# Four of the eleven bits of a Hadamard transform: from a TensorE product with 16×16 blocks to sums and differences of row chunks on VectorE

## The chip, the cores and the metric

The kernel runs on one core of a Trainium2 chip. A core has five engines, each with its own queue of instructions that it works off in order: TensorE (PE in the profile; its weight loads are PEld), VectorE (DVE), ScalarE (ACT), GpSimd (POOL) and SyncE (SP, which here only issues DMAs). They wait for each other by semaphores. TensorE reads SBUF and writes PSUM; eight PSUM banks are used. The metric is the time of one execution on the device in microseconds (us). Everything is computed in fp32; one fp32 product is two TensorE instructions in the trace.

## The reference

Four sequences of 512 rows with 512 columns go through a gated linear scan and then through a feed-forward network, each between two layer norms and with a residual. What matters here is the second half:

```python
up_gate = jnp.einsum('bsd,hd->bsh', x, W1)
up_lin = jnp.einsum('bsd,hd->bsh', x, W3)
hidden = jax.nn.silu(up_gate) * up_lin
hidden = fwht(hidden)               # Walsh-Hadamard, 2048 values, times 1/sqrt(2048)
out = jnp.einsum('bsh,dh->bsd', hidden, W2)
```

`hidden` has 2048 columns. The transform is a symmetric 2048×2048 matrix of plus and minus ones, the Kronecker product of eleven 2×2 matrices, one for each bit of the column number.

## The kernel before

**The transform goes into the weights.** Because the transform is linear, the kernel never transforms `hidden`. It transforms the rows of w2 (2048×512) once and multiplies the untransformed `hidden` with the result. It does so in two steps. `transform_high` (line 639): rows are loaded as `(p r)`, so that partition p holds rows 16p to 16p+15, and a product with the 128×128 Hadamard matrix `h_sb` does the seven bits of p for each of 16 values of r; ScalarE copies each result back into the piece (line 644), and GpSimd's queue stores the piece in a DRAM scratch `w2_h` (line 646). `load_w2` loads it in eight pieces of two values of r; odd pieces lie in buffers of the pool `stream2`, even ones in buffers of the tag `ht`. `transform_low` (line 661): `load_low(m)` fetches rows back so that 128 consecutive rows lie on 128 partitions, and a product with `h16_sb`, a block-diagonal matrix of eight 16×16 Hadamard matrices, does the four low bits. It handles a tile m (0 to 7, two blocks of 128 rows, one of the top half of the rows and one of the bottom half) as two products of 512 columns, `g` in the profile (line 672), each followed by a scaled eviction by ScalarE (line 673).

**Seven products instead of eight.** Every matrix product is done by Winograd's form of Strassen's scheme on 2×2 blocks: seven products in the order P1, P2, P6, P5, P7, P3, P4 (`ORDER`, line 31). The sums of blocks are formed beforehand on VectorE: `combine_left` (line 124) makes S1 to S4, `combine_right` (line 131) makes T1 to T4, four operations each. P6 needs S2 and T2, P5 needs S1 and T1, P7 needs S3 and T3, P3 needs S4, P4 needs T4. A combined weight tile has seven blocks of 128×256 (896 KB over the partitions). `kept` (line 138) stores it in DRAM through GpSimd's queue, and later sequences load it from there (`again`, line 147).

**Units and filling.** The work is a row of units. `attn_unit(b, u)` with u = 0, 1, 2 does three projections of sequence b for the scan, `ffn_unit(b, m)` with m = 0 to 7 does 128 columns of both halves of w1 and w3 and makes `ht`, one eighth of `hidden`. Each unit is seven products (`project`, line 424), written into three PSUM banks X, Y and Z: P1, P6, P7 and P4 add up in X, P2 goes to Y, P5 and P3 to Z. ScalarE copies P1, P6, P5 and P4 out, VectorE adds Y after P2, X after P7 and Z after P3 (`seven`, line 392). Between the products of a unit, `run` (line 101) takes one step from the queue `fill`: after P2, P5, P3 and P4, or after every product where the unit is `dense`. The steps are products of other work: `attn_out(b)` (with the weight `wo`, tile names y, and with the gated output `og` as the left side), `ffn_out(b, part)` (with w2, tile names po; a part is two tiles m), the transposes of the next input, and here the `h` and `g` products of w2's transform. The ffn units of the first sequence are dense.

**Order on the engines.** TensorE's and SP's queues are in the order in which the program is written (line 82). The queues of VectorE, ScalarE and GpSimd are ordered by a scheduler when the kernel is built: by priority (`URGENT`, `SOON`) and by `behind(what)`, which puts work behind an earlier instruction. For each unit of the first sequence `combine_weights` makes S1 to S4 of the next unit's w1 and w3 on VectorE (eight operations), behind the unit's P7.

**Buffers.** `stream` has five buffers and holds wi, wf, wg, w1 and w3. `stream2` has four, taken in turn by pieces 1, 3, 5, 7 of w2, then `wo` (two tiles, first for sequence 0, then loaded again for sequence 1) and the tiles of w2. A load waits on SP's queue until the earlier user of its buffer is done, and every later load on that queue waits with it. For the first sequence too, w2's transformed tiles are stored and then loaded again, by `load_down_w` (line 550).

Of the kernel before, what the change touches and what calls it, by code (L numbers as in the profile page):

```python
# [11 lines left out]
F32 = mybir.dt.float32  # L12
AF = mybir.ActivationFunctionType
ALU = mybir.AluOpType
P = 128
# [11 lines left out]
S3 = A21  # L27
B11, B21, B22, B12, T1, T2, T4 = range(7)
T3 = B12

ORDER = (
    ("P1", A11, B11, "X", True),
# [10 lines left out]
def kernel(  # L43
# [14 lines left out]
    nc = tc.nc  # L58
# [2 lines left out]
    NT = T // P  # L61
    ND = D // P
    NF = FF // P
    NU = NF // 2
    NS = 2
    H = T // 2
# [18 lines left out]
    def bank(name):  # L85
        return psum.tile([P, 2, H], F32, tag="ps", name=name)
# [44 lines left out]
    def combine_right(t, eng):  # L131

        eng.tensor_sub(t[:, T1], t[:, B12], t[:, B11])
        eng.tensor_sub(t[:, T2], t[:, B22], t[:, T1])
        eng.tensor_sub(t[:, T3], t[:, B22], t[:, B12])
        eng.tensor_sub(t[:, T4], t[:, B21], t[:, T2])
# [7 lines left out]
    def stream_tile(key, b, pool=stream):  # L144
        return pool.tile([P, 7, H], F32, tag="w", name="_".join(map(str, (*key, b))))
# [39 lines left out]
        ffn_w[b, m] = weight(w1, "w1", m, b), weight(w3, "w3", m, b)  # L185


    h_sb = const.tile([P, P], F32, tag="had", name="had")
    nc.sync.dma_start(out=h_sb, in_=had)
    h16_sb = const.tile([P, P], F32, tag="had16", name="had16")  # L190
    nc.gpsimd.memset(h16_sb, 0.0)
    gn_sb = const.tile([P, ND], F32, tag="gn", name="gn")

    def load_constants():
        nc.gpsimd.dma_start(out=gn_sb, in_=gnorm.rearrange("(c p) -> p c", p=P))
        for g in range(P // 16):
            nc.gpsimd.dma_start(out=h16_sb[ts(g, 16), ts(g, 16)], in_=had[0:16, 0:16])

    ident = const.tile([P, P], F32, tag="ident", name="ident")
    make_identity(nc, ident)  # L200
# [10 lines left out]
    def behind(what):  # L211


        return tc.issue_after(read[what].ins)
# [339 lines left out]
    def ffn_out(b, part):  # L554

        ms = range(part * NS, (part + 1) * NS)
        w = {m: down_w.pop((b, m)) for m in ms}

        def multiply(ps, a, bb, first):
            if b not in outs:  # L560
                outs[b] = work.tile([P, 2, 2, D], F32, tag="wide", name=f"f_{b}", bufs=3)
            for t in range(2):
                for m in ms:
                    nc.tensor.matmul(  # L564
                        ps[:, t, :], hts[b, m][:, a, ts(t, P)], w[m][:, bb, :],
                        start=first and t == 0 and m == ms[0], stop=m == ms[-1],
                        skip_group_check=True,
                    )

        norm = {}  # L570

        end = b == B - 1 and ms[-1] == NU - 1
        held = []

        def done(i, j, tile=None):
            if not norm:
                norm[0] = OutputNorm(b, outs[b], EPS, "f")
            with tc.high_priority(offset=SOON * i):
                norm[0].quarter(i, j, (0, 1) if tile is None else (tile,))
            if j == 1 - i and tile != 0:  # L580
                norm[0].half(i, held if end else None)
                if end and i == 0:
                    return
                if end:
                    with tc.issue_after(norm[0].last.ins):
                        for residual in held:
                            residual()
                for t in range(0 if end else 2 * i, 2 * i + 2):
                    if b < B - 1:
                        eng = nc.gpsimd  # L590
                    else:
                        eng = nc.scalar if t == NT - 2 else nc.sync
                    eng.dma_start(out=out[b, ts(t, P), :], in_=xs[b][:, t, :])

        return seven(
            f"po_{b}_{part}", multiply, lambda i, j: outs[b][:, i, :, ts(j, H)],
            done if ms[-1] == NU - 1 else None, add=part > 0, by_tile=end,
        )
# [19 lines left out]
            combine_right(w[c], nc.vector)  # L618
            kept(("wo", c), w[c])

    NR = FF // P
    NJ = NR // 2
    w2_h = scratch.tile([P, NR, D], F32, tag="w2h", name="w2_h")
    w2_p = []

    def load_w2(pieces):
        for j in pieces:
            if j % 2:
                t = stream2.tile([P, 2, D], F32, tag="w", name=f"w2p_{j}")
            else:  # L630
                t = work.tile([P, 2, D], F32, tag="ht", name=f"w2p_{j}", bufs=4)
            for k in ((0, 1), (1, 2)) if j == 0 else ((0, 2),):
                nc.sync.dma_start(
                    out=t[:, k[0] : k[1], :],
                    in_=w2.rearrange("(p r) f -> p r f", r=NR)[:, 2 * j + k[0] : 2 * j + k[1], :],
                )
            w2_p.append(t)

    def transform_high(j, k):

        p = psum.tile([P, D], F32, tag="ps", name=f"h_{j}_{k}")
        t = w2_p[j]
        nc.tensor.matmul(p, h_sb, t[:, k, :], start=True, stop=True)  # L643
        nc.scalar.copy(t[:, k, :], p)  # L644
        if k == 1:
            nc.gpsimd.dma_start(out=w2_h[:, 2 * j : 2 * j + 2, :], in_=t)

    low_w = {}

    def load_low(m):  # L650
        low_w[m] = stream_tile(("w2", m), 0, stream2)
        for n, blocks in enumerate(((B11, B12), (B21, B22))):
            row = n * (NF // 2) + m
            nc.sync.dma_start(
                out=low_w[m][:, blocks[0] : blocks[1] + 1 : blocks[1] - blocks[0]],
                in_=w2_h.rearrange("p r f -> (p r) f")[ts(row, P), :].rearrange(
                    "p (n f) -> p n f", n=2
                ),
            )

    def transform_low(m):

        def make(k):
            w = low_w[m]
            if k == 0 and m + 2 < NU:
                load_low(m + 2)
            blocks = ((B11, B12), (B21, B22))[k]
            t = w[:, blocks[0] : blocks[1] + 1 : blocks[1] - blocks[0]]  # L670
            p = bank(f"g_{m}_{k}")
            nc.tensor.matmul(p, h16_sb, t, start=True, stop=True)  # L672
            nc.scalar.mul(t, p, 1.0 / FF**0.5)
            if k == 1:
                combine_right(w, nc.vector)
                kept(("w2", m), w)

        return [partial(make, k) for k in range(2)]


    def high(j0, j1):
# [26 lines left out]
    attn_unit(0, 0, True)  # L708
    with behind("P2"):
        combine_weights(2)  # L710
    attn_unit(0, 1)
    with behind("P3"):
        with tc.high_priority(offset=URGENT):
            combine_weights(2)
        with tc.high_priority(offset=SOON):
            apply = [normalize_tiles(1, "a", i, 2, True) for i in (0, 2)]
    wo_t[0] = load_wo()
    load_attn_w(1, 0)
    while fill:
# [13 lines left out]
    load_attn_w(1, 1)  # L733
    fill.extend([None] * 3 + attn_out(0))
    attn_unit(1, 0, True)
    load_low(0)
    load_low(1)
    load_attn_w(1, 2)
    fill.extend(transform_low(0) + transform_low(1))
    attn_unit(1, 1, True)  # L740
    load_ffn_w(0, 0)
    fill.extend(transposes(0, "f"))
    attn_unit(1, 2)
    with behind("P7"):
        combine_weights()
    for b in range(B):
        last = b == B - 1
        for m in range(NU):
            if m + 1 < NU:
                load_ffn_w(b, m + 1)  # L750
            if b == 0 and m % NS == 0:
                for k in range(m + 2, min(m + 2 + NS, NU)):
                    fill.extend(transform_low(k))
            if m == 0 and not last:
                fill.extend([None] * 4 * (b > 0) + attn_out(b + 1))
            if m and m % NS == 0:
                if last and m == NU - NS:
                    fill.extend([None] * 8)
                fill.extend([None] + ffn_out(b, m // NS - 1))
            if m % NS == 1:  # L760
                load_down_w(b, m // NS)
            if m == 2 and b == 0:
                load_x(2)
            if m == 4 and b + 2 < B:
                with behind("P7"):
                    late = [normalize_tiles(b + 2, "a", i, 2, True) for i in (0, 2)]
            if m in (4, 5) and b + 2 < B:
                for t, k in enumerate((3, 5) if m == 4 else (0, 3)):
                    beside[k] = [partial(behind_copy, partial(late[m - 4], range(t, t + 1)))]
            if m == 6 and not last:  # L770
                load_fold(*((b + 2, "a") if b + 2 < B else (b + 1, "f")))
            if m == NU - 1 and not last:
                transpose_fold(*((b + 2, "a") if b + 2 < B else (b + 1, "f")))
            ffn_unit(b, m, b == 0)
            with behind("P7"):
                combine_weights()
        tail = ffn_out(b, NU // NS - 1)
# [54 lines left out]
```

## Time and profile before

| what | value |
|---|---|
| three runs | 833.66, 834.70, 837.85 us; median 834.7 us |
| the profiled execution | 833.4 us, its span from first to last instruction 831.6 us |
| TensorE | busy 814.6 us, mean granted clock 0.996 |
| VectorE / ScalarE / GpSimd | busy 459.8 / 267.9 / 69.2 us |
| `h` products, line 643 | 16 calls (32 instructions), 5.3 to 48.5 us |
| `g` products, line 672 | 16 calls (32 instructions), 96.6 to 209 us |
| evictions of `g`, line 673 | 16, 588 ns each, 9.2 us |
| HBM read / written | 125.90 / 42.99 MB |

"Busy" is the time in which an engine had an instruction running. Instructions overlap at their ends: an addition of 128×512 values on VectorE has a duration of 0.69 us, but in a row of independent ones the next starts 0.605 us after the one before; for 128×256 it is 0.42 and 0.335 us, for a 128×256 fp32 product on TensorE 0.379 us per instruction with a start every 0.216 us. In the timelines below the columns are: start in us, length in us, engine, line, operation, what it writes and reads, shapes, how many instructions are merged into the row, and in brackets the idle time before it and what ended it. In the text, "pitch" is the time from start to start.

### The profile page before, as it was taken

The page shows a single profiled execution, that of the slowest core. Times are in us where ns is not written, and L with a number is a line of the kernel's source. Part 1 is how long each engine was busy: PE and PEld are TensorE (multiplying, and loading weights), DVE is VectorE, ACT ScalarE, POOL GpSimd, SP SyncE. Part 2 cuts the span into 40 slices and gives each one's busy share as a digit, 9 for nine tenths or more (in the row PEclk, how much of TensorE's full clock was granted, in tenths as well). Part 3 has the DMA queues.
Part 4 walks back from the last instruction along what each step waited for, and adds up shares of the span by engine and source line. Part 5 has one row for each costly group of instructions (what it writes and reads, how often), then busy time and mean ns, then how long its engine had stood idle before and what let it go on. Part 6 is the DMA issues. An engine that isn't in the chain of part 4 may idle for free.

```text
span 831.6 us, 9833 instructions
## 1 busy us (share of the span) xinstructions
PE 814.6 (98%) x3728; PEld 702.2 (84%) x3728; DVE 459.8 (55%) x926; ACT 267.9 (32%) x380; POOL 69.2 (8%) x112
## 2 busy tenths in 40 slices
PE   7999999999999999999999999999999999999995
PEld 4788888888888888888888888888888888888884
DVE  5486787766547657357236645637246334524345
ACT  4554463432321135235421133425221111322111
POOL 4120111111100001002000000102000000100000
PEclk9999999999999999999999999999999999999998
DMA  9996369696978435736455533825363642625201
GB/s 334 414 399 231 99 205 360 216 398 219 374 221 304 149 118 224 291 136 258 185 145 205 156 115 127 331 98 203 122 232 101 241 177 89 228 106 205 78 11 50
DMA packets 65743, 169.54 MB, mean 204 GB/s; under 512 B 4768, under 2 KB 40224, under 8 KB 65696
## 3 DMA queue, kind: packets, MB, share of 16 engines
q1 hardware_dynamic: 56528, 125.65, 43.0%
q0 software_dynamic: 8448, 41.96, 12.6%
q10 hardware_dynamic: 720, 1.31, 0.4%
q8 instruction: 29, 0.48, 0.2%
q14 instruction: 18, 0.15, 0.1%
HBM read 125.90 MB, written 42.99 MB: 203 GB/s over the span
## 4 chain that ended last, share of the span: by engine, by line
PE 93%; DVE 4%; ACT 1%; issue 1%; DMA 0%; POOL 0%; POOLq 0%; DVEq 0%; SPq 0%; ACTq 0%
PE X_f L431 25%; PE Z_f L431 13%; PE X_po L564 13%; PE X_a L431 10%; PE Z_po L564 7%; PE Y_f L431 6%; PE Z_a L431 5%; PE X_y L517 3%; PE Y_po L564 3%; PE Y_a L431 3%; PE h L643 2%; PE Z_y L517 2%; PE g L672 1%; PE Y_y L517 1%; DVE x L321 1%
## 5 line engine op out<-in xcount | busy, mean ns | idle before, releaser
L431 PE MATMUL X_f<-xt_f,w 128*128 128x256 f32 x1024 | 241.7, 379 | 0.5 <-ACT d_f L418 0.3
L431 PEld LDWEIGHTS X_f<-xt_f,w 128*128 128x128 f32 x1024 | 194.1, 190 | 30.2 <-issue 2.9
L418 ACT COPY d_f<-X_f 128x512 f32<-128x512 f32 x96 | 56.1, 584 | 294.6 <-PE X_f L431 259.3
L431 PE MATMUL Z_f<-xt_f,w 128*128 128x256 f32 x512 | 121.1, 379 | 0.2 <-ACT d_f L418 0.2
L564 PE MATMUL X_po<-w,ht 128*128 128x256 f32 x512 | 120.9, 379 | 0.2 <-DVE f L416 0.2
L431 PEld LDWEIGHTS Z_f<-xt_f,w 128*128 128x128 f32 x512 | 97.2, 190 | 15.1 <-issue 0.7
L564 PEld LDWEIGHTS X_po<-w,ht 128*128 128x128 f32 x512 | 97.2, 190 | 13.7 <-DVE f L416 0.6
L416 DVE TENSOR_TENSOR f<-X_po,f 128x512 f32<-128x512 f32 x51 | 35.2, 689 | 98.2 <-PE X_po L564 91.7
L446 DVE TENSOR_TENSOR ht<-d_f 128x1024 f32<-128x1024 f32 x32 | 39.0, 1218 | 61.2 <-ACT d_f L540 47.5
L564 PE MATMUL Z_po<-w,ht 128*128 128x256 f32 x256 | 60.5, 379 | 0.0
L431 PE MATMUL Y_f<-xt_f,w 128*128 128x256 f32 x256 | 60.5, 379 | 0.0
L431 PEld LDWEIGHTS Y_f<-xt_f,w 128*128 128x128 f32 x256 | 48.6, 190 | 7.9 <-issue 0.7
L564 PEld LDWEIGHTS Z_po<-w,ht 128*128 128x128 f32 x256 | 48.6, 190 | 6.6
L418 ACT COPY d_a<-X_a 128x512 f32<-128x512 f32 x36 | 21.0, 584 | 87.2 <-PE X_a L431 70.8
L225 POOL TENSOR_TENSOR rs_f<-rs_f,power 128x2 f32<-128x2 f32 x16 | 14.0, 878 | 405.0 <-DVE nm_f L313 383.4
L416 DVE TENSOR_TENSOR d_f<-X_f,d_f 128x512 f32<-128x512 f32 x32 | 22.1, 691 | 31.8 <-PE X_f L431 31.8
L540 ACT ACTIVATE d_f<-d_f 128x1024 f32<-128x1024 f32 x32 | 33.8, 1055 | 0.9
L431 PE MATMUL X_a<-xt_a,wi 128*128 128x256 f32 x128 | 33.1, 381 | 0.8 <-ACT w2p L644 0.7
L416 DVE TENSOR_TENSOR d_f<-Z_f,d_f 128x512 f32<-128x512 f32 x32 | 22.0, 688 | 20.6 <-PE Z_f L431 20.6
L416 DVE TENSOR_TENSOR f<-Z_po,f 128x512 f32<-128x512 f32 x28 | 19.2, 686 | 24.9 <-PE Z_po L564 24.9
L431 PE MATMUL X_a<-xt_a,wf 128*128 128x256 f32 x128 | 32.8, 379 | 0.0
L431 PEld LDWEIGHTS X_a<-xt_a,wi 128*128 128x128 f32 x128 | 23.9, 190 | 8.9 <-issue 3.1
(154 smaller groups left out, 1008.0 us busy)
## 6 DMA issues: line engine op xcount, KB each, us to landing
w<-s_w SPq DMA_DIRECT2D x80, 896.0 KB, 6.4
s_w<-w POOLq DMA_DIRECT2D x24, 896.0 KB, 6.7
w<-in_W_dram SPq DMA_DIRECT2D x32, 256.0 KB, 6.5
wi<-s_wi SPq DMA_DIRECT2D x6, 896.0 KB, 10.8
wf<-s_wf SPq DMA_DIRECT2D x6, 896.0 KB, 7.0
wg<-s_wg SPq DMA_DIRECT2D x6, 896.0 KB, 6.0
wo<-s_wo SPq DMA_DIRECT2D x6, 896.0 KB, 10.3
w_h<-w2p POOLq DMA_DIRECT2D x8, 512.0 KB, 8.2
```

Source lines behind the costliest of these rows:

```text
L225: read["power"] = nc.gpsimd.tensor_tensor(r, r, power_t[:, 0:n], ALU.pow)
L321: nc.vector.scalar_tensor_tensor(x_t, self.y[:, i, t, :], r[:, t : t + 1], x_t, ALU.mult, ALU.add)
L416: read[what] = nc.vector.tensor_add(to, ps[which], to)
L418: read["copy"] = nc.scalar.copy(to, ps[which])
L431: nc.tensor.matmul(ps[:, n, :], w[:, a, c, :], xt[:, bb, c, :], start=first and n == 0 and c == 0, stop=c == 1, skip_group_check=True,)
L446: nc.vector.tensor_mul(to.rearrange("p (t k) f -> p k t f", t=2), a.rearrange("p k (t f) -> p k t f", t=2), b2.rearrange("p k (t f) -> p k ...
L517: nc.tensor.matmul(ps[:, t, :], og[:, a, c, ts(t, P)], w[c][:, bb, :], start=first and t == 0 and c == 0, stop=c == 1, skip_group_check=True,)
L540: nc.scalar.activation(d[:, 0], d[:, 0], AF.Silu)
L564: nc.tensor.matmul(ps[:, t, :], hts[b, m][:, a, ts(t, P)], w[m][:, bb, :], start=first and t == 0 and m == ms[0], stop=m == ms[-1], skip_g ...
L643: nc.tensor.matmul(p, h_sb, t[:, k, :], start=True, stop=True)
L672: nc.tensor.matmul(p, h16_sb, t, start=True, stop=True)
```

## The change

Rows of w2 are now taken as `(r p)`: chunk r (0 to 15) is 128 consecutive rows, and partition p is the row's place in it. The product with `h_sb` stays; its eviction now carries the scale. The four remaining bits are those of the chunk number r, and a bit is transformed by adding and subtracting whole chunks. Two bits are done in the pieces, before the store to `w2_h` (`butterfly(g)`: pieces 2g and 2g+1, which hold four chunks, eight operations of 128×512 on VectorE); they get a third slot of space for it. The third bit is done between the two tiles of a part (`low_pair`, four operations of 128×512). The fourth is done between the two halves of a tile, together with the sums T1 to T4 (`low_tile`, five operations on VectorE and one on ScalarE), so that block B12 is never made. `h16_sb`, its memset, its eight small loads and all `g` products are gone.

The tiles' blocks stand in another order, `W2`, for which `ffn_out` looks them up. The first sequence's `ffn_out` uses the tiles in place: `load_low(p)` loads both tiles of a part at the top of units 1, 3, 5 and 6, and `low_pair` and the two `low_tile` are recorded in the same unit at P5, P3 and P4, behind P2, P7 and P3. The last part lies in the buffer of `og`. The ffn units of the first sequence are no longer dense, and two numbers of empty fill steps differ.

```diff
+W2 = 0, 4, 5, 3, 6, 2, 1
...
-    h16_sb = const.tile([P, P], F32, tag="had16", name="had16")
-    nc.gpsimd.memset(h16_sb, 0.0)
...
-        for g in range(P // 16):
-            nc.gpsimd.dma_start(out=h16_sb[ts(g, 16), ts(g, 16)], in_=had[0:16, 0:16])
...
-                        ps[:, t, :], hts[b, m][:, a, ts(t, P)], w[m][:, bb, :],
+                        ps[:, t, :], hts[b, m][:, a, ts(t, P)], w[m][:, W2[bb], :],
...
+    w2_rows = w2.rearrange("(r p) f -> p r f", p=P)
+    def chunks(j):
+        r = NU * (j // 4) + j // 2 % 2 + 4 * (j % 2)
+        return slice(r, r + 3, 2)
     def load_w2(pieces):
...
-                t = stream2.tile([P, 2, D], F32, tag="w", name=f"w2p_{j}")
+                t = stream2.tile([P, 3, D], F32, tag="w", name=f"w2p_{j}")
...
+            rows = w2_rows[:, chunks(j), :]
...
-        nc.scalar.copy(t[:, k, :], p)
-        if k == 1:
-            nc.gpsimd.dma_start(out=w2_h[:, 2 * j : 2 * j + 2, :], in_=t)
...
+        nc.scalar.mul(t[:, k, :], p, 1.0 / FF**0.5)
+    def butterfly(g):
+        x, y = w2_p[2 * g], w2_p[2 * g + 1]
+        nc.vector.tensor_add(x[:, 2], x[:, 0], y[:, 0])
+        nc.vector.tensor_sub(y[:, 0], x[:, 0], y[:, 0])
+        nc.vector.tensor_add(x[:, 0], x[:, 1], y[:, 1])
+        nc.vector.tensor_sub(y[:, 1], x[:, 1], y[:, 1])
+        nc.vector.tensor_add(x[:, 1], x[:, 2], x[:, 0])
+        nc.vector.tensor_sub(x[:, 2], x[:, 2], x[:, 0])
+        nc.vector.tensor_sub(y[:, 2], y[:, 0], y[:, 1])
+        nc.vector.tensor_add(y[:, 1], y[:, 0], y[:, 1])
+        for k, t in enumerate((x, y)):
+            nc.gpsimd.dma_start(out=w2_h[:, chunks(2 * g + k), :], in_=t[:, 1:3])
+    def load_low(p):
+        ms = range(p * NS, (p + 1) * NS)
+        if p == 3:
+            pair = work.tile([P, NS, 7, H], F32, tag="og", name="w2_67")
+            tiles = [pair[:, k] for k in range(NS)]
+        else:
+            tiles = [stream_tile(("w2", m), 0, stream2) for m in ms]
+        for n, k in ((1, 4), (0, 0)):
+            for m, t in zip(ms, tiles):
+                nc.sync.dma_start(
+                    out=t[:, k : k + 2].rearrange("p k f -> p (k f)"),
+                    in_=w2_h[:, n * NU + m, :],
+                )
+        for m, t in zip(ms, tiles):
+            down_w[0, m] = t
+    def low_pair(p):
+        x, y = (down_w[0, m] for m in range(p * NS, (p + 1) * NS))
+        for k, to in ((4, 2), (0, 4)):
+            nc.vector.tensor_add(x[:, to : to + 2], x[:, k : k + 2], y[:, k : k + 2])
+            nc.vector.tensor_sub(y[:, to : to + 2], x[:, k : k + 2], y[:, k : k + 2])
+    def low_tile(m):
+        t = down_w[0, m]
+        nc.vector.tensor_add(t[:, W2[B11]], t[:, 4], t[:, 2])
+        nc.vector.tensor_sub(t[:, 4:6], t[:, 4:6], t[:, 2:4])
+        nc.vector.scalar_tensor_tensor(
+            t[:, W2[T2]], t[:, 3], -2.0, t[:, W2[B11]], ALU.mult, ALU.add
+        )
+        nc.scalar.mul(t[:, W2[T3]], t[:, 3], -2.0)
+        nc.vector.tensor_sub(t[:, W2[T4]], t[:, W2[B21]], t[:, W2[T2]])
+        nc.vector.tensor_sub(t[:, W2[T1]], t[:, W2[B22]], t[:, W2[T2]])
+        kept(("w2", m), t)
+    def low_steps(p):
+        def step(what, make, at):
+            with behind(what):
+                make(at)
+        for k, what, make, at in (
+            (3, "P2", low_pair, p), (5, "P7", low_tile, 2 * p), (6, "P3", low_tile, 2 * p + 1)
+        ):
+            beside.setdefault(k, []).append(partial(step, what, make, at))
...
     with behind("P2"):
         combine_weights(2)
+        butterfly(0)
+        butterfly(1)
     attn_unit(0, 1)
...
             apply = [normalize_tiles(1, "a", i, 2, True) for i in (0, 2)]
+        butterfly(2)
...
     attn_unit(1, 0, True)
-    load_low(0)
-    load_low(1)
+    with behind("P7"):
+        butterfly(3)
     load_attn_w(1, 2)
-    fill.extend(transform_low(0) + transform_low(1))
...
-    fill.extend(transposes(0, "f"))
+    fill.extend([None] + transposes(0, "f"))
...
+    LOW = 1, 3, 5, 6
     for b in range(B):
         last = b == B - 1
         for m in range(NU):
+            if b == 0 and m in LOW:
+                load_low(LOW.index(m))
+                low_steps(LOW.index(m))
             if m + 1 < NU:
                 load_ffn_w(b, m + 1)
-            if b == 0 and m % NS == 0:
-                for k in range(m + 2, min(m + 2 + NS, NU)):
-                    fill.extend(transform_low(k))
             if m == 0 and not last:
-                fill.extend([None] * 4 * (b > 0) + attn_out(b + 1))
+                fill.extend([None] * (4 if b else 2) + attn_out(b + 1))
...
-            if m % NS == 1:
+            if b and m % NS == 1:
                 load_down_w(b, m // NS)
...
-            ffn_unit(b, m, b == 0)
+            ffn_unit(b, m)
```

## The prediction

> **What bounds the kernel now.** I read the page's busy shares and its chain of waits first, then TensorE's timeline, then VectorE's.
>
> ```profile
> PE 814.6 (98%) x3728; PEld 702.2 (84%) x3728; DVE 459.8 (55%) x926; ACT 267.9 (32%) x380; POOL 69.2 (8%) x112
> ...
> PE 93%; DVE 4%; ACT 1%; issue 1%; DMA 0%; POOL 0%; POOLq 0%; DVEq 0%; SPq 0%; ACTq 0%
> ```
>
> TensorE holds 93% of the chain, DMA nothing. A busy TensorE need not be at its peak, so I went through the starts of all its instructions: after the first 20 us a next one comes 0.216 us after a 128×256 instruction almost everywhere. The exceptions over 0.06 us between 60 and 200 us sum to 1.6 us.
>
> ```profile
> 119.31 1.02 PE L672 MATMUL g<-w,had 128*128 128x512 f32 x2
> 120.17 1.89 PE L431 MATMUL Y_f<-xt_f,w 128*128 128x256 f32 x8
> 121.90 1.02 PE L672 MATMUL g<-w,had 128*128 128x512 f32 x2
> 122.76 1.03 PE L431 MATMUL X_f<-xt_f,w 128*128 128x256 f32 x4
> 124.01 1.13 PE L431 MATMUL X_f<-xt_f,w 128*128 128x256 f32 x4 [0.23 <-DVE w L127]
> ```
>
> Two things are to be seen. A `g` call takes 0.86 us of TensorE (119.31 to 120.17), a product of a unit 1.73. And the second weight of P6 in unit 0 comes 0.5 us late (124.01, where 122.76+0.86 was due): it waits for VectorE's S2, line 127. VectorE is already late here, though 55% busy over the span:
>
> ```profile
> 45.00:75.00 30.00, 29.88 (x142) 25.42 (x141) 28.12 (x59) 16.67 (x23) 5.36 (x7) 1.00 0.95 365
> 75.00:95.00 20.00, 20.00 (x98) 17.72 (x97) 10.04 (x20) 7.51 (x11) 0.71 (x1) 1.00 0.14 47
> 95.00:118.00 23.00, 23.00 (x107) 18.83 (x106) 19.94 (x50) 12.90 (x22) 3.17 (x5) 1.00 0.58 195
> 118.00:137.00 19.00, 18.77 (x79) 14.71 (x78) 18.10 (x38) 8.70 (x12) 3.19 (x6) 1.00 0.89 332
> ```
>
> These are windows: length, busy time of PE, PEld, DVE, ACT and POOL with counts, granted clock, DMA share, GB/s. VectorE is full from 45 to 75 us and nearly so from 118 to 137.
>
> **Removed.** 16 `g` calls × 0.855 = 13.7 us of TensorE, all on the path. Their 16 evictions (9.2 us of ScalarE), 32 sums of 128×256 on VectorE (8×4×0.335 = 10.7 us), eight 896 KB loads and GpSimd's eight small ones lie beside the path and count nothing.
>
> **Added.** On VectorE, by pitch: butterflies 32×0.605 = 19.4 us, `low_pair` 16×0.605 = 9.7, `low_tile` 8×(0.605+3×0.335+0.39) = 16.0. An operation on 256 values with a scalar is not in the trace; it lies between the plain sum (0.335) and the 512-value one of line 321 (0.66), and I take 0.39, since the sum has the same size. Net +34 us, which costs only where something in VectorE's queue is awaited by TensorE. I walked that queue in the changed kernel's own order, with durations from the trace, against TensorE's products at 1.73 us.
>
> *The gated output of sequence 1's first unit.* `butterfly(2)` stands in the full stretch:
>
> ```profile
> 60.92 0.76 DVE L355 COPY xt_a<-pt_a 128x256 f32<-128x256 f32 x2
> 62.39 1.42 DVE L355 COPY xt_a<-pt_a 128x256 f32<-128x256 f32 x4 [0.72 <-PE pt_a L348]
> ...
> 64.33 1.22 DVE L446 TENSOR_TENSOR og<-o,d_a 128x1024 f32<-128x1024 f32 x1
> ...
> 67.87 1.22 DVE L446 TENSOR_TENSOR og<-o,d_a 128x1024 f32<-128x1024 f32 x1
> ...
> 69.82 1.89 PE L517 MATMUL X_y<-wo,og 128*128 128x256 f32 x8
> ```
>
> From 53 us on there is one gap, 0.72 us. Eight operations × 0.605 = 4.84; less 0.72; plus 0.4, because the second normalization's scalars (which wait for GpSimd's power, 0.9 us behind 53.2) now stand ahead of the scan: the second half of `og` is written at 69.1+4.5 = 73.6. The first of `X_y`'s four calls (0.43 us) needs only the first half, so TensorE loses 73.7−(69.82+0.43) = **3.45 us**.
>
> *Attention unit 2 of sequence 1, and ffn unit 0.* Three `g` calls between 94.9 and 102.7 used to cover a chain of normalizations. Without them P6 of the unit is due at 94.9+5×1.73 = 103.5, but X can be overwritten only after ScalarE's copy of P1, which stands behind two xn (from the scalars at 99.29: to 100.95), two line-316 (102.2), the X copy (102.75) and the tanh of line 459 (103.8), and ends at 104.35: **0.85 us**. Unit 0 then starts at 115.0 on this scale. VectorE's second scan there ends at 111.5 (xn to 106.85, X copy, line 462 to 108.5, scan, two copies of pt, scan), then X add, four sums, Z add and four copies to 115.4, T1, a sum, T2 to T4 to 118.3, `og`, Y add, `og` to 121.15, S2 at 121.6. P6's second weight is due at 115.0+2×1.73+0.86 = 119.3: **2.3 us**, where 0.5 was lost before.
>
> *Units 2, 4, 6 and 7.* They follow the units with low steps, whose operations stand ahead of the next unit's eight sums. Unit 2, from the end of y's P7 in unit 1: add 0.6, `ht` 1.13, two statistics 0.7, four sums 1.34, Y add 0.6, three sums 1.0, y's Z add 0.6, S2 0.42, with 0.2 of starting 6.6; TensorE has P1, P2 and y's P3, 5.2: 1.4 late. The second weight's S2 comes 2.25 later, over statistics, sums and small operations; P6's first half lasts 0.86: 1.25 more, **2.65** together. In the same way unit 4 (copy, silu, then 7.0 us of queue = 8.9, against four products and a half = 7.77) **1.15**; unit 6 (6.5 against 6.04) **0.5**; unit 7 (7.15 against 6.04) **1.1**. Bounds for these four: nothing, if the other gaps of VectorE absorb it; 9.7+16.0−8.0 = 17.7 us, the loop's whole net addition, if none does. I take 5.4, by the walk, which finds gaps of several us before the X add in unit 1 and in unit 4.
>
> *Edits at nothing.* Loads and stores in 2 KB runs instead of 4 KB (pieces) or 1 KB (low rows) change DMA, which the chain shows at 0%. Butterflies 0 and 1 run in VectorE's idle time from 23.6 to 36 us and end at 31.9 and 34.4; their stores (8.2 us to landing at the median before) free the buffers of `wo` at 40 to 43, where its loads were issued at 40.05 to 43.40 and landed 6 us later. VectorE needs them at 57: 7 us of cover, without which the X add would wait behind `prepare_wo`. On SP's queue the attention weights behind `wo` have 7 us too. `butterfly(3)` lies in the idle 5.4 us before 83.04. The low rows of parts 1 and 2 are loaded when y's or po's P4 frees their buffers, some 13 us before `low_pair`; such loads landed in 3.0 to 9.7 us. They fit; if late, `low_pair` holds VectorE's queue and the X add behind it, so P4. Two fill steps more or fewer only shift products.
>
> **Sum.** −13.7 + 3.45 + 0.85 + 2.3 + 2.65 + 1.15 + 0.5 + 1.1 = −1.7; the waits of before in these places outside the first go with it (0.09, 0.49, 0.08, 0.47): **−2.8 us**. The profiled execution took 833.4 (span 831.6, 1.8 around it): 830.6. The median of the runs shown, 834.7, is 1.3 above it: **831.9 us**.
>
> A new kind of gap is the 2.6 us before `og`: the longest of before after the start, 0.85 us at 18.56, left the granted clock at 1.00. From the trace alone the price of a cold clock is 2.2 us: the first five instructions of `h` ran 0.43 us longer each than the later ones. One rule of the Trainium skill speaks against the change here: "TensorE: Matmul & The Clock Gate" (Part 1) says that about 3.4 us of idling halves TensorE's clock until it has been busy for as long again. By it the sum stays as it is, and a gap over that length would add some 1.7 us (an estimate, half of the 3.4); no gap of this trace is long enough to test it.
>
> **Rivals.** *The gain is mostly kept.* If VectorE's queue is less tight in the loop and only the first place and 0.85+2.3 cost: −13.7+6.6−0.6 = −7.7, 827.0; with only the first place −10.2, 824.5. For it: 133 of 188 us of VectorE are busy from 45 to 233, so on average there is room. Against: the order of the changed queue, in which no later gap helps an S2.
> *VectorE becomes the bound in the first sequence's ffn units.* One place, the S2 in the units after low steps. With no gap absorbing anything the loss is 17.7 instead of 5.4: 844.2. It turns to slower (over 838.9) once these four units lose more than 5.4+7.0 = 12.4 us. For it: 18.1 of 19 us busy in 118 to 137 before; against: 7.0 of 19 in 176 to 195 and 9.1 in 214 to 233.
> *It doesn't do what it says*, as the saved products were waited out anyway: a `g` call did stand where a chain ran (95 to 103), 3×0.86; the rest stands in a dense row of products. Then 834.7.
>
> **How the numbers follow.** Forecast 0.52, gain kept 0.24, VectorE the bound 0.18, nothing 0.06. A measurement tells about 0.5% (4.2 us) from nothing. The forecast's own spread, 828 to 836, passes −4.2 us with about a third of its chance: faster 0.24+0.17 = 0.41, within 0.5% 0.35+0.06 = 0.41, slower 0.18. Range 825.5 to 839: from the rival with little loss to the loop losing 12.4; outside lie about 0.08 below and 0.12 above. The forecast's own range is 828 to 836.
>
> **What would show it.** Right: no `g` rows; TensorE at some 801 us busy; waits of `X_y` on `og` of line 446 near 71 us, and of P6 in units 0, 2, 4, 6 and 7 on the sum that makes S2. Wrong: those waits absent, or several times longer; `low_pair` waiting for a DMA; a granted clock under 1.00 after 71 us.

## The result and the profile after

The changed kernel took 834.6 us (median of 20 runs, 832.0 to 835.6), the kernel before 834.1 us (20 runs, 833.1 to 837.9) in the same comparison: a ratio of 0.9999 with a 95% interval of 0.999 to 1.0008. It makes no difference that can be told, though 16 products of TensorE are gone. The profiled execution has a span of 832.6 us, where the kernel before had 831.6.

The page of the changed kernel, with the lines that answer to those shown of before: the busy times, the shares of the chain of waits by engine, and two groups of products (busy us, mean ns; then TensorE's idle time just before them and what ended most of it).

```profile
PE 806.2 (97%) x3696; PEld 696.7 (84%) x3696; DVE 492.8 (59%) x982; ACT 262.5 (32%) x372; POOL 67.0 (8%) x103
...
PE 82%; DVE 10%; DMA 3%; ACT 2%; issue 1%; SPq 0%; POOL 0%; POOLq 0%; DVEq 0%
...
L431 PE MATMUL X_f<-xt_f,w 128*128 128x256 f32 x1024 | 243.7, 380 | 7.2 <-DVE w L130 6.9
...
L517 PE MATMUL X_y<-wo,og 128*128 128x256 f32 x128 | 30.8, 381 | 2.7 <-DVE og L446 2.0
```

VectorE's share of the chain has grown from 4% to 10%, TensorE's has fallen from 93% to 82%, and a DMA has come in with 3%. TensorE is busy 8.4 us less than before, not 13.7: 2.5 us more went into work at a lower clock (the half rate and the start in the table below), and most of the rest is a matter of counting, since an instruction ahead of a wait counts as busy for 0.379 us and one that is followed at once for 0.216. The idle time is named: 6.9 us ahead of `X_f` (a product of an ffn unit) until VectorE's line 130, which makes S2 of a weight, and 2.0 us ahead of `X_y` until `og`.

To see where the time went I took the starts of all TensorE instructions again and counted what lay beyond 0.216 us per 128×256 instruction. The work itself went from 809.2 to 795.4 us, 13.8 less; the time beyond it went from 6.7 to 22.4 us, 15.7 more. By place (us, after less before):

| place | foreseen | measured |
|---|---|---|
| 62 to 75 us: a transpose, P6, `X_y` | 3.45 | 3.1 |
| P6 of attention unit (1,2) | 0.8 | 0.8 |
| P6 of ffn unit 0 | 1.8 | 2.1 |
| half rate right behind it | 0 | 1.7 |
| P6 of ffn units 2, 4, 6, 7 | 4.9 | 5.0 |
| `X_y` of sequence 2, at 340 us | 0 | 0.8 |
| cold clock at the start, to 20 us | 0 | 0.8 |
| small gaps, each under 0.25 | 0 | 1.5 |

The first product starts 0.3 us earlier, the last one ends 1.7 us later. TensorE's timeline after (start, length, engine, line, operation, count, and in brackets the idle time before a group and who ended it) shows the foreseen waits:

```profile
72.24 0.67 PE L517 MATMUL X_y<-wo,og 128*128 128x256 f32 x2 [0.65 <-DVE og L446]
74.29 0.92 PE L517 MATMUL X_y<-wo,og 128*128 128x256 f32 x3 [1.38 <-DVE og L446]
...
125.90 1.13 PE L431 MATMUL X_f<-xt_f,w 128*128 128x256 f32 x4 [2.32 <-DVE w L130]
126.86 3.42 PE L431 MATMUL Z_f<-xt_f,w 128*128 128x256 f32 x8
...
163.84 1.10 PE L431 MATMUL X_f<-xt_f,w 128*128 128x256 f32 x4 [1.43 <-DVE w L130]
165.69 1.13 PE L431 MATMUL X_f<-xt_f,w 128*128 128x256 f32 x4 [0.75 <-DVE w L130]
...
340.67 1.56 PE L517 MATMUL X_y<-wo,og 128*128 128x256 f32 x6 [0.62 <-DMA wo<-s_wo]
```

The first pair is the wait on `og`, the second lies in ffn unit 0, the third in unit 2, and the last row is the wait of sequence 2 for `wo`. The row at 126.86 holds eight instructions in 3.42 us, where eight take 1.89 elsewhere. The windows of the changed kernel (length, TensorE busy with its count, granted clock, DMA share, GB/s) show why:

```profile
74.30:77.70 3.40, 3.40 (x16) 1.00 0.64 270
...
127.00:130.40 3.40, 3.40 (x10) 0.51 0.98 406
```

From 127.0 to 130.4 us the granted clock is 0.51, right behind the wait in unit 0; behind the waits on `og` it stays at 1.00. The lost 0.8 us at 340 us has its origin on SP's queue; first before, then after (start, length, queue, line, what is loaded):

```profile
322.35 1.76 SPq L120 DMA_DIRECT2D x<-in_x_dram  x4
...
325.10 0.93 SPq L149 DMA_DIRECT2D wo<-s_wo  x2
```

```profile
326.17 1.76 SPq L123 DMA_DIRECT2D x<-in_x_dram  x4
...
328.93 0.92 SPq L152 DMA_DIRECT2D wo<-s_wo  x2
```

The loads of sequence 3's `x` wait for the buffer that sequence 0's output leaves; that output was ready 3.8 us later (its last stores are issued at 323.04 instead of 319.21), which I put down to the ffn units of sequence 0: they no longer take a step off the list behind every product. No run tried that edit, or the two numbers of empty fill steps, by itself. `wo` for sequence 2 stands behind these loads on the queue and came 3.8 us later too, which was too late for `X_y`.

### The profile page after: what moved, and what is told of

It is laid out like the page before. It is cut to its first block, busy times and chain, and to the rows that moved or that the text cites. A ratio compares the mean times of both kernels' runs of the same rounds, so it can differ in the third digit from the quotient of the medians.

```text
span 832.6 us, 9764 instructions
## 1 busy us (share of the span) xinstructions
PE 806.2 (97%) x3696; PEld 696.7 (84%) x3696; DVE 492.8 (59%) x982; ACT 262.5 (32%) x372; POOL 67.0 (8%) x103
## 4 chain that ended last, share of the span: by engine, by line
PE 82%; DVE 10%; DMA 3%; ACT 2%; issue 1%; SPq 0%; POOL 0%; POOLq 0%; DVEq 0%
PE X_f L431 23%; PE Z_f L431 12%; PE X_po L564 12%; PE X_a L431 7%; PE Z_po L564 6%; PE Y_f L431 5%; PE Z_a L431 4%; PE X_y L517 3%; PE Y_po L564 3%; PE Y_a L431 2%; PE h L646 2%; PE Z_y L517 1%; DMA wo<-s_wo 1%; PE Y_y L517 1%; DVE f L416 1%
## 5 line engine op out<-in xcount | busy, mean ns | idle before, releaser
L564 PEld LDWEIGHTS X_po<-w,ht 128*128 128x128 f32 x512 | 97.2, 190 | 13.8 <-DVE f L416 0.6
L517 PE MATMUL X_y<-wo,og 128*128 128x256 f32 x128 | 30.8, 381 | 2.7 <-DVE og L446 2.0
```

Source lines behind the costliest of these rows:

```text
L517: nc.tensor.matmul(ps[:, t, :], og[:, a, c, ts(t, P)], w[c][:, bb, :], start=first and t == 0 and c == 0, stop=c == 1, skip_group_check=True,)
L564: nc.tensor.matmul(ps[:, t, :], hts[b, m][:, a, ts(t, P)], w[m][:, W2[bb], :], start=first and t == 0 and m == ms[0], stop=m == ms[-1], sk ...
```

## The experiments

My theory after the result: the gain is real and is given back in waits of TensorE on what VectorE's queue does too late, in a handful of places. The order of the queue would decide, not the amount of work in it. Rivals: VectorE has too much to do (volume), or the `g` products had filled time in which TensorE would have waited anyway (cover). Every ratio below is against the kernel before in the same comparison, with its 95% interval; where I turn a ratio into us, it is times 833.6.

**Without g.**

```
-            p = bank(f"g_{m}_{k}")
-            nc.tensor.matmul(p, h16_sb, t, start=True, stop=True)
-            nc.scalar.mul(t, p, 1.0 / FF**0.5)
+            nc.scalar.mul(t, t, 1.0 / FF**0.5)
```

> The kernel before, with the 16 products g left out (the lower four bits of w2's transform are not computed; ScalarE scales the loaded rows in place); VectorE's work is that of before. Theory (the 13.8 us of TensorE were a real gain, and the changed kernel gives them back in VectorE's queue): 13.8 less, and only the waits that need no butterfly and no low step come back: P6 of sequence 1's third attention unit (0.8) and P6 of ffn unit 0 (2 to 3.5), so about 10 us less than before, 824. Rival (the g calls only filled time in which TensorE waited anyway): within 1.5 us of before, with the same time lost in gaps that g filled.

Measured: 829.33, ratio 0.9956 (0.9942 to 0.9971), 4 us less instead of 10. Beyond the start, six waits between 70 and 170 us sum to 8.5 us (1.15, 1.59, 0.59, 2.25, 0.61, 2.32). That spoke for the rival, but the first and the last are the experiment's own: for the first, the copy that TensorE awaits stands behind three of the scalings. For the last, ScalarE's timeline in this run:

```profile
167.79 0.63 ACT L671 ACTIVATE w<-w 128x512 f32<-128x512 f32 x1 [3.83 <-DMA w<-w_h]
168.33 0.57 ACT L418 COPY d_f<-Z_f 128x512 f32<-128x512 f32 x1
```

ScalarE sat 3.83 us until the DMA of the low rows, since no product of TensorE stood ahead of the scaling any more; the Z copy that frees a bank is queued behind it, and TensorE waits for that copy. The waits are those of the profiled execution, the fastest of eight (827.8 us, mean granted clock 0.997); the other seven have 0.992 to 0.994, so the median of 829.33 probably holds some time at a lower clock that this profile does not show. The run is not a clean test, so it was made again with a narrow `g`, below.

**One butterfly earlier.**

```
     with behind("P2"):
         combine_weights(2)
         butterfly(0)
         butterfly(1)
+        butterfly(2)
...
-        butterfly(2)
```

> The changed kernel with butterfly(2) behind the other two, some 20 us earlier. Theory (place in VectorE's queue): the waits of TensorE between 62 and 74 us (0.39 before pt, 0.60 before P6, 2.36 at X_y) go, all but 0.3: 3 us less than the changed kernel, about 831.5; the waits in the ffn units stay as they are. Rival (volume: VectorE has too much to do in the first sequence, wherever it stands): the wait moves to another product before 120 us and less than 1 us is gained.

Measured: 831.29, ratio 0.9968 (0.9956 to 0.998): 2.6 us less than the changed kernel. The waits between 60 and 75 us fell from 3.35 to 0.80, and the later ones stayed to within about 0.1 us. TensorE's timeline of this run has all eight instructions of `X_y` in one row, without a wait:

```profile
70.83 1.89 PE L517 MATMUL X_y<-wo,og 128*128 128x256 f32 x8
```

All of VectorE's work is still done, 20 us earlier. So it was the place.

**Sums of the weights first.**

```
-    with behind("P7"):
+    with behind("P7"), tc.high_priority(offset=URGENT):
         combine_weights()
...
             ffn_unit(b, m)
-            with behind("P7"):
+            with behind("P7"), tc.high_priority(offset=URGENT):
                 combine_weights()
```

> The changed kernel with the eight sums of each ffn unit's weights raised in the scheduler's priority, ahead of ht, statistics and low steps, in the first sequence alone. Theory (order): the waits of P6 on S2 go: 2.5 in unit 0 to about 0.3, and with it the 1.5 us at half rate behind it; 2.5 in unit 2, 1.2 in unit 4, 0.6 in unit 6, 1.2 in unit 7; up to 1 us of new waits: 8 us less than the changed kernel, about 826.5. Rival (volume): the sums of the hidden tile or the adds that free a bank become late instead, and less than 3 us is gained.

Measured: 826.36, ratio 0.9909 (0.9896 to 0.9922): 7.5 us less than the changed kernel. The waits on S2 are gone in all five units, and with them the phase at half rate; a wait of 1.25 us in unit 0 is new (for a ScalarE copy that stands behind the squares of `o`), and where `X_y` of sequence 2 had waited 0.8 us there are now 1.8, at 329 and 333 us, for a tile of the ffn weights and for `wo`. What the edit does is seen in VectorE's timeline ahead of unit 4; first the changed kernel, then this run:

```profile
196.57 1.22 DVE L446 TENSOR_TENSOR ht<-d_f 128x1024 f32<-128x1024 f32 x1 [1.27 <-ACT d_f L540]
...
200.32 0.68 DVE L416 TENSOR_TENSOR d_f<-Y_f,d_f 128x512 f32<-128x512 f32 x1
...
201.59 0.42 DVE L129 TENSOR_TENSOR w<-w 128x256 f32<-128x256 f32 x1
...
202.53 0.67 DVE L416 TENSOR_TENSOR f<-Z_po,f 128x512 f32<-128x512 f32 x1
203.12 0.41 DVE L130 TENSOR_TENSOR w<-w 128x256 f32<-128x256 f32 x1
```

```profile
195.54 0.42 DVE L130 TENSOR_TENSOR w<-w 128x256 f32<-128x256 f32 x1
...
196.55 0.69 DVE L416 TENSOR_TENSOR d_f<-Y_f,d_f 128x512 f32<-128x512 f32 x1
```

In the changed kernel the second weight's S1 (201.59) and S2 (203.12) stand behind `ht` and its sums, statistics, and the adds of P2 (200.32) and of `po` (202.53). VectorE idles at none of them: from 196.57 to 203.12 each operation follows the one before at its pitch. It begins this row late, since `ht` waits for ScalarE, and the sum that TensorE needs first stands near the row's end. With the priority raised all sums of both weights (the last three from 195.54 on) stand ahead of the add at 196.55.

**Sequence 3's x later.**

```
-            if m == 2 and b == 0:
-                load_x(2)
+            if m == 2 and b < 2:
+                load_x(b + 2)
...
-            if b + 3 < B:
-                load_x(b + 3)
```

> The changed kernel with the load of sequence 3's x issued some units later, so that it no longer stands on SP's queue ahead of the load of wo for sequence 2. Theory (the 0.8 us wait of X_y at 339.7 us is an x load waiting for the stores of sequence 0's output, which end 3.8 us later than before, with wo queued behind it): that wait goes, 0.8 less, about 833.8. Rival (wo is late because its own transfer is slow, or because the DMA engines are full): the wait stays between 0.5 and 1.

Measured: 833.03, ratio 0.9989 (0.998 to 0.9998), 0.8 us less than the changed kernel. The two intervals overlap, so the time alone shows little, but there is no wait at `X_y` of sequence 2 in the trace. The windows of this run have a surprise:

```profile
73.70:77.10 3.40, 3.33 (x8) 0.53 0.64 270
...
127.00:130.40 3.40, 3.34 (x16) 1.00 0.97 376
```

The half rate now lies behind the waits on `og`, which are as long as before, and not behind the wait in unit 0 (again 2.48 us, from 124.58 to 127.06), where the clock stays at 1.00. The last section says why.

**The three moves together.**

> The three moves together: butterfly(2) early, the sums of the ffn weights first, x of sequence 3 loaded later; all work of the changed kernel is kept. Theory (order in queues, so the gains add): 3.3 and 8.2 by the two runs that moved these alone, 1 to 1.5 by the wait of X_y near 332 us: 834.6 - 12.7 = about 822. Rival (VectorE's volume, so that what one move gains the next gives back): 826 or more, no better than the sums alone.

Measured: 821.30, ratio 0.9851 (0.9837 to 0.9864), 12.3 us less than the changed kernel, where the three alone sum to 10.9. The page of this run:

```profile
PE 801.7 (98%) x3696; PEld 695.9 (85%) x3696; DVE 492.8 (60%) x982; ACT 262.3 (32%) x372; POOL 67.4 (8%) x103
...
PE 90%; DVE 5%; DMA 2%; ACT 1%; issue 1%; POOL 0%; POOLq 0%; SPq 0%; DVEq 0%
...
L431 PE MATMUL X_f<-xt_f,w 128*128 128x256 f32 x1024 | 241.9, 379 | 0.3 <-ACT d_f L418 0.3
```

The same operations as in the changed kernel, VectorE as busy (492.8 us), and TensorE's span of work is 13.0 us shorter: the time beyond its work is 9.4 us instead of 22.4. VectorE's volume does not stand against the gain.

**Narrow g, at its old place.** TensorE still gates the queues as before, but for 13 us less work.

```
-            nc.tensor.matmul(p, h16_sb, t, start=True, stop=True)
-            nc.scalar.mul(t, p, 1.0 / FF**0.5)
+            nc.tensor.matmul(p[:, 0, 0:32], h16_sb, t[:, 0, 0:32], start=True, stop=True)
+            nc.scalar.mul(t[:, 0, 0:32], p[:, 0, 0:32], 1.0 / FF**0.5)
```

> The kernel before with each g on 32 columns instead of 512 and its eviction as narrow, at its old place in every queue (the lower four bits of w2's transform are computed for 32 of 512 columns alone). The run that left g out let ScalarE's queue wait for the DMA of the low rows, with the copies that free a bank behind it (waits of 1.1 and 2.3 us); here TensorE still gates them. Theory (13 us of TensorE are a gain, and what comes back are the waits of P6 in the third attention unit and in ffn unit 0, 3 to 5 us): 8 to 10 us less than before, 824 to 826. Rival (g covered chains of the first sequence everywhere): 829, as in that run.

Measured: 832.31, ratio 0.9987 (0.9968 to 1.0005): a miss. One place took nearly all of the gain. TensorE's and VectorE's timelines in ffn unit 0:

```profile
127.23 2.08 PE L431 MATMUL X_f<-xt_f,w 128*128 128x256 f32 x4 [5.99 <-DVE w L127]
```

```profile
125.63 1.22 DVE L479 TENSOR_TENSOR o<-o 128x1024 f32<-128x1024 f32 x1
126.77 0.41 DVE L127 TENSOR_TENSOR w<-w 128x256 f32<-128x256 f32 x1
```

S2 of the second weight (line 127 in this kernel, at 126.77) had been placed behind `og`'s four sums and the square sums. In the kernel before it stands ahead of three of them:

```profile
123.53 0.42 DVE L127 TENSOR_TENSOR w<-w 128x256 f32<-128x256 f32 x1
```

TensorE lost 6.2 us there and some 3 more at half rate.

**Without the low steps.** `low_pair` and `low_tile` lose their operations on VectorE and ScalarE; GpSimd writes zeros into the blocks that they would make.

> The changed kernel without low_pair's and low_tile's operations on VectorE and ScalarE (the lower bits two to four and the right-hand combinations of w2 are left out; GpSimd fills the blocks with zeros), loads and stores kept. Theory (the added VectorE work stands ahead of the sums): the waits of P6 in units 2, 4, 6 and 7, 5.4 us, go; those of unit 0 and at X_y stay: 829.2. Rival (these waits come from g's missing cover, the adds and statistics alone being late): more than half of the 5.4 us stays, 832 or more.

Measured: 832.41, ratio 0.9984 (0.9976 to 0.9993), 1.3 us less than the changed kernel instead of 5.4. TensorE's timeline in units 2 and 4:

```profile
163.11 1.10 PE L431 MATMUL X_f<-xt_f,w 128*128 128x256 f32 x4 [0.41 <-DVE w L130]
165.35 1.13 PE L431 MATMUL X_f<-xt_f,w 128*128 128x256 f32 x4 [1.14 <-DVE w L130]
...
202.87 1.13 PE L431 MATMUL X_f<-xt_f,w 128*128 128x256 f32 x4 [0.99 <-DVE w L130]
```

The waits on S2 are still there: 1.9 us in unit 2 (2.5 with the low steps), 1.16 in unit 4 (the same), 0.56 in unit 6 (0.59); only that of unit 7 went (1.15). Of 5.4 us the low steps made 1.8; the other 3.6 are there without them. In unit 4 VectorE's queue from `ht` to that S2 has the same operations in the same order in both runs. This is the rival's outcome.

**The same priority in the kernel before**, as a control.

> A control: the kernel before with the same raised priority of the ffn weights' sums. Theory (the g products cover those waits, so there is little to gain without the change): only the 0.8 us that the kernel before loses at S2 (0.39 and 0.37) can go, 833 or no difference that can be told. Rival (the order is worth its 8 us in any kernel, and the change has no part in it): 826.

Measured: 834.64, ratio 1.0014 (1.0005 to 1.0023). The wait on S2 in unit 0 (0.39) went, and others came or grew: 1.5 us at 36.5, 0.8 at `X_y`, and the 0.37 in unit 2, which was one ahead of a Z product and not on S2, became 1.0. These are the waits of the profiled execution, the slowest of eleven (836.4 us), and the one at 36.5, for a load of w2, lies far ahead of the first unit that the edit touches; what the run shows is its median. The order is worth nothing where the `g` products are.

**Narrow g again, and with the order.** The run that was to have narrow `g` and the raised priority was given the kernel of narrow `g` alone, so what its expectation says of the order was not tried in it; it repeats that kernel (831.91, ratio 0.998, 0.9971 to 0.9989).

> The kernel before with narrow g (as in the run of that name) and the sums of the ffn weights first. Theory (that run lost its gain at one place, where the scheduler put S2 of ffn unit 0's second weight behind og's sums: 6.2 us, and 3.0 at half rate behind it): both go, about 823.5. Rival (g covered chains everywhere): 829 or more.

The run after it had both edits:

> The kernel before with narrow g and the sums of the ffn weights first (the run that was to be this one repeated the narrow g without the order). Theory (the narrow g lost its gain at one place, where S2 of ffn unit 0's second weight stood behind og's sums: 6.2 us, and 3.0 at half rate behind it): both go, about 823.5. Rival (g covered chains everywhere): 829 or more.

Measured: 823.99, ratio 0.9885 (0.9871 to 0.9898). The 6.2 us and the half rate are gone, and 9.6 us of the 13 are kept, with VectorE's work that of before. The theory holds: what looked like cover everywhere was for the most part one sum in one queue.

**The squares in halves**, on top of the three moves.

```
-            nc.scalar.activation(o, o, AF.Square)
+            for m in range(2):
+                nc.scalar.activation(o[:, m], o[:, m], AF.Square)
```

> The version with the three moves, and the squares of o as two halves on ScalarE, so that the Z copy of ffn unit 0 stands behind 1 us less. Theory: of the 1.25 us that TensorE waits at 124 us for that copy, 0.9 goes: 820.4. Rival (the copy is late for its own operand): no difference.

Measured: 820.82, ratio 0.9846 (0.9832 to 0.9859), which can't be told from the three moves' 0.9851. The wait of 1.25 us for the Z copy is gone, but the X copy now stands behind the first half of the squares, for which P7 waits 0.4 us, and 1.7 us at `X_y` behind it are new, where 0.35 were. The span is the same, 819.6.

**Unit 0 alone.** The priority raised for the weights of ffn unit 0 and no others.

> The changed kernel with the priority raised for the weights of ffn unit 0 alone. Theory: the 2.5 us wait on S2 at 123 us goes but for 0.3, and the phase at half rate (1.5 to 1.7 us) behind it with it; the waits in units 2, 4, 6 and 7 stay: 830.5 to 831. Rival (the half rate belongs to the kernel and not to this wait): it shows up behind another wait, and only 2.2 us is gained, 832.4.

Measured: 832.55, ratio 0.9989 (0.998 to 0.9998): the rival's number, though the interval leaves room for the theory's. In the profiled execution the wait on S2 went, the 1.25 us for the ScalarE copy came, and the half rate appeared behind the waits on `og` (granted clock 0.50 from 75.0 to 78.1 us).

## Why the prediction was right, and where it was not

The forecast was 831.9, the measured time 834.6, inside its range; that the change would hardly show came out, and for the main reason given. The small gain of 2.8 us did not: no difference can be told. The places that were foreseen sum to 11.0 us in both columns of the table above, so that agreement is no luck of terms that cancel; 4.8 us were not foreseen.

*Removed.* 13.7 us of TensorE foreseen, 13.8 measured. Two readings are a little off: the second weight that comes "0.5 us late" at 124.01 is 0.39 late by its own row (the start after it is 0.1 late again), and in unit 2 a sum 2.25 later less a half of 0.86 is 1.4, not 1.25. Each moves the forecast by 0.2 us at most.

*The gated output.* 3.45 us foreseen, 3.35 measured, though 1.0 of it came earlier than at `X_y`, before a transpose and a P6. That `butterfly(2)` in the full stretch is the cause is shown by moving it.

*Attention unit 2 and ffn unit 0.* 0.85 and 2.3 us foreseen, 0.79 and 2.48 measured. That S2's place in the queue makes the second is shown by the sums put first, in all units and in unit 0 alone. The first was touched by no run and stays in all versions with the change.

*Units 2, 4, 6 and 7.* 2.65, 1.15, 0.5 and 1.1 foreseen, 2.50, 1.16, 0.59 and 1.15 measured. The sizes are right and the reason is not. The prediction put them down to low steps that "stand ahead of the next unit's eight sums". Without the low steps two thirds stay: they are made by the other queue entries that the walk had counted (`ht`, statistics, adds on TensorE's own products), which were there before, while the `g` products gave them time. In unit 7 alone the low steps are the whole of it. Already the trace after says so for unit 4: VectorE is idle for 1.27 us at 196.57, so the low steps ahead of it are over. A walk through a queue gives the time of a wait, and not which of its entries to blame.

*No cold clock.* This step failed. The prediction left the granted clock at 1.00, since no gap would reach 3.4 us; behind one of 2.48 us it fell to 0.51, which cost 1.7 us, the price that the prediction had put on a longer gap. A granted clock under 1.00 after 71 us was one of its own signs of being wrong, and TensorE's busy time, to be some 801 us, came out as 806.2.

*Edits at nothing.* No wait over 0.3 us in the first sequence, after the start, ended with a DMA. But that shifted products cost nothing was wrong ("two fill steps more or fewer only shift products"; that the ffn units are no longer dense got no price at all): an output came 3.8 us later, which through a buffer and SP's queue cost 0.8 us one sequence further on; the later load of `x` removed it. Which of these edits made it late was not tried.

The half rate (1.7) and this 0.8, with 0.8 us more of cold clock at the start, 1.5 us of small gaps and an earlier first product (0.3), make up the 4.5 us between the walk's −2.8 and the +1.7 at the last product. The start is not the change's: two kernels that keep the old beginning lost 1.6 and 3.0 us to the cold clock there.

*The rivals.* VectorE as the bound is refuted by the three moves, which keep all its work. "Does nothing, as the products were waited out anyway" has the right time for the wrong reason: with the queue in order 12.3 of the 13.8 us are kept. What is true of it is that the `g` products hid a bad order. Left open: what the 0.79 us in attention unit (1,2) and the small gaps would take to go.

## What to carry to other kernels

Taking work off the engine that bounds a kernel also takes away the time in which other queues caught up: after such a change, look for the operations that the bounding engine awaits and that stand behind others which nothing needs so soon, and move those first. Test that with an edit of order alone, once with the change and once without it; here it was worth 7.5 us with it and nothing without. And when time moves inside one stage, follow its last output through the buffers and queues into the next.

## What the runs showed of the hardware

A wait far shorter than expected can cost TensorE's clock, and not always. The same 2.48 us wait in ffn unit 0 was followed by half rate (0.427 us per instruction) in the profiled executions of the changed kernel, of the early butterfly and of the run without low steps, and by full rate in the run with the later `x`; there, and in the run with unit 0 alone, the half rate came behind the waits on `og`, 2.35 us of idling within 2.9 us. The run with all sums first had the same waits on `og` and no half rate at all.

The traces show what decides. In that of the changed kernel the granted clock goes to full at 11.00 us, to half at 127.05, to full at 130.47 and to half at 826.78, behind the last product: 34, 1 and 204 times 3.413 us apart. In all 14 traces the changes lie on such a grid, with an offset of its own in each. I cut each trace along its grid and summed TensorE's idling in every step of 3.413 us, that is, the time beyond 0.216 us per instruction. Of the steps at full rate each with 2.2 us of it or more was followed by half rate, and none with 2.1 or less; the limit is known no finer than that. Two steps each, first of the changed kernel, then of the run with the later `x` (length, TensorE busy with its count, granted clock, DMA share, GB/s):

```profile
123.64:127.05 3.41, 1.15 (x5) 1.00 0.94 299
127.05:130.46 3.41, 3.41 (x9) 0.50 1.00 412
```

```profile
125.11:128.53 3.42, 1.47 (x7) 1.00 0.90 287
128.53:131.94 3.41, 3.41 (x18) 1.00 1.00 411
```

In the changed kernel nearly the whole wait of unit 0 lies in one step, with 2.4 us of idling. In the run with the later `x` a step ends inside that wait, at 125.11, and the step behind it holds 2.05 us; there it is the waits on `og` that lie in one step together, with 2.4. An episode lasted one step and cost 1.7 us. Behind the 6.2 us wait of the narrow `g` the granted clock was 0.50 for three steps, to 133.42, the last 6.2 us of them with work. Of the changed kernel's 20 executions two have a mean granted clock of 0.997 (832.0 and 833.1 us) and the others 0.992 to 0.995; the profiled one has 0.994, so an episode is probably the rule there.

The Trainium skill's page "TensorE: Matmul & The Clock Gate" (Part 1) says that the clock is judged over a window of about 3.4 us that runs freely, and that it falls after an idle one. The grid fits a freely running window of that length; that the window must be idle throughout does not fit, since 2.2 us of idling in it were enough.
